# A new order for the work of a two-layer graph kernel: constants of the written-out plan changed

## The chip, the cores and the metric

The kernel runs on one core of a Trainium2 chip. The metric is the device time of one execution in microseconds (us). The core has five engines, each with its own queue that is worked off in order: PE (TensorE, matrix products), ACT (ScalarE), DVE (VectorE), POOL (GpSimd) and SP (SyncE, which here only issues DMA transfers). An engine that reaches an instruction whose inputs are not ready waits, and all that is queued behind it waits too.

## The reference

The input x has 128 batches of 128 tokens with 512 features, in float32. Two layers follow each other:

```python
# layer 0: graph maximum, residual, layer norm
A = einsum('od,bdn->bon', adj, x);  C = A + b            # per batch: adj @ x
out = max over the last axis of relu((C - A)[..., None] + A[:, :, None, :])   # one value a row
x = layernorm(x + out)
# layer 1: masked attention over the graph, projection, layer norm, residual, layer norm
q, k, v = x @ w_qkv                                      # 8 heads of 64
attn = softmax(where(adj == 0, -inf, q @ k.T / 8))
o = (attn @ v) @ w_proj + b_proj
x = layernorm(x + o + (layernorm(o) * gamma + beta))
```

Because both weights of layer 0 are adj, C - A is the bias, and the maximum over a row is relu(rowmax(adj @ x) + b).

## The kernel before

**Tiles and stages.** Batches go through in groups of four, 32 groups in all. For one batch, a tile of 128 x 512, the stages are these, with the engine and the line of the profile.

Layer 0: `load_x` (SP, L91), `conv` (PE, L186, the product with adj), `conv_max` (DVE, L190), `relu_0` (POOL, L196), then either `stats_x` (DVE, L233/L234) with `rstd_x` and `shift_x` (POOL, L240 to L250), or `add_0` and `stats_0` (ACT, L202 and L523) with `rstd_0` and `shift_0` (POOL, L213 to L225), and `norm_0` (ACT L259, or DVE L257).

Transposing x: `x_halves` splits each float into two 16-bit planes (ACT, L271) and stores them to DRAM (SP, L273, tile rowsx); `crossbar_x` reads them back with a transposing DMA (SP, L277). The tile xplanes has one buffer, so that the next `x_halves` waits for the store of the last. The four batches of the first group are transposed on PE instead (L266) and copied or split from there. `copy_x` (DVE L308 or ACT L310), `product_v` (PE, L316, in plain float32) and `keep_v` (ACT, L319) make v for batches 0 and 1.

Products in three terms: float32 operands are kept in three forms h, l and d. `split` makes the high part and l on DVE (L288, L290), `split_high` makes h (POOL L295 or ACT L297) and `split_d` makes d = h - l (POOL or DVE, both L302). Weights are split likewise by `split_w` (DVE, L150 to L152) and `split_w_rest` (ACT, L159/L160), in 16 parts (w0 to w15) that `load_w` brings in. A product then is eight matmuls of h and l (L336, L337) into one PSUM bank and four of d (L344) into another. `dense` makes q and k (indices 4 to 11) and v (0 to 3) of a group; `dense_main` (ACT, L371) and `dense_rest` (DVE, L375) add the two banks up.

Layer 1: `scores` (PE, L391), `masked` (DVE, L407), `row_max` (DVE, L416), `exps` (ACT, L425, eight instructions with their sums), `weights` (DVE, L433/L434), `halves` (ACT L440, then a store by SP, L444) and `crossbar_T` (SP, L449, a transposing DMA into eT), `attend` (PE, L471), `heads` (the split of the result o into oh, ol and od, by the lines of `split`), `project` (PE, L336 to L344), `projected_main` (DVE, L503), `projected_rest` (DVE, L517). Then the residual: a second load of x into xb (`residual`, SP, L490), `residual_x` (POOL, L494/L495) which applies the first layer's norm to it again, `residual_o` (POOL or DVE, L512). `stats` (ACT L523, POOL L529 to L538) serves both norms, `norm_1` is on DVE (L542, L517), `norm_2` on ACT (L550) with the store of the result by SP (L551). The last group transposes its softmax weights on PE (`transpose_e`) and copies them with ACT (`weights_T`, L462).

**The order.** PE's order is written out: lists of stages for the prologue, for each group and for the tail (`pro_order`, `dense_order`, `pair_order`, `tail_order`). A group's period has its q and k products first, then alternates attention of the group, v products of the group, projections of the group before, and `conv` of a group to come. Each PE stage has a length in `LENGTH`, and so a planned time. Every other stage gets a planned time as an offset from a PE stage, taken from the table `O`: four numbers, one for each batch of a group, the same for all groups in the middle; `pro` holds the times of the prologue, `tail`, `last` and `final` those of the last two groups. Flags under `two` choose between two engines or, for `project` and `dense`, between two kinds of PSUM buffer (four single banks, ps_1; two double banks, ps_2, which the scores use too). All stages are sorted by planned time and issued in that order on each engine; the planned times themselves do nothing else.

```python
at(u + O["main"][j], ...)        # a stage: planned time, function, arguments
plan.sort(key=lambda p: p[:2])   # issued in this order on every engine
```

Buffers add waits: xplanes and planes have one buffer each, e and o have three, eT, xh and xb two. A batch number in a tile's name is given by the trace where the tile belongs to one batch by name (pp_(10, 0), the product 0 of group 10; xh_('o', 36), a split of o of batch 36); tiles such as xt, xplanes, eT and e carry no number there. In this document a stage's number is its batch, and in the steady period called group 10 (from 623.43 us) the batches 36 to 39 are projected, 40 to 43 scored, and 44 to 47 normed and transposed for the next period.

Of the kernel before, what the change touches and what calls it, by code (L numbers as in the profile page):

```python
# [26 lines left out]
def tile_adj_resnorm_d2(  # L27
# [519 lines left out]
    def norm_2(b):  # L547
# [6 lines left out]

    plan, pe = [], {}
    LENGTH = dict(T=0.87, x=0.44, S=0.95, AV=0.93, conv=0.87, dense=2.82, po=2.82)
    O = {'add_0': [-38.7, -4.55, -0.42, -31.04],
 'conv_max': [2.74, 1.55, 6.27, 8.56],
 'dense_order': [('dense', 4), ('dense', 5), ('conv', 3), ('conv', 2), ('dense', 6), ('dense', 8),
                 ('dense', 7), ('dense', 11), ('dense', 10), ('dense', 9)],  # L560
 'final': {'norm_1': [5.56, 13.1, 10.45, 9.62],
           'norm_2': [10.36, 42.75, 85.51, 29.81],
           'residual': [-12.36, -9.08, -4.53, -8.07],
           'residual_o': [4.55, 8.68, 6.6, 3.13],
           'residual_x': [-31.86, -65.51, -7.05, -41.27],
           'stats_1': [5.32, 6.68, 6.06, 7.2],
           'stats_2': [7.33, 15.86, 26.2, 12.18]},
 'last': {'norm_1': [10.51, 11.91, 8.79, 8.49],
          'norm_2': [13.32, 18.89, 14.16, 15.4],
          'residual': [1.83, -2.16, 5.46, -20.9],  # L570
          'residual_o': [3.49, 5.23, 7.41, 5.77],
          'residual_x': [-44.3, 7.6, -14.48, -29.96],
          'stats_1': [3.85, 7.55, 7.55, 5.02],
          'stats_2': [10.52, 13.02, 12.74, 12.77]},
 'load': [-20.41, 3.65, -32.28, -8.94],
 'main': [4.11, 3.12, -0.15, 0.25, 3.8, -0.35, 5.39, -1.68, -0.18, -1.25, -0.35, -0.17],
 'norm_0': [13.43, 36.38, -3.62, 0.76],
 'norm_1': {'norm_1': [12.75, 21.79, 12.88, 17.03],
            'norm_2': [19.25, 33.88, 24.66, 29.53],
            'residual': [-18.48, -24.43, 1.31, 4.46],  # L580
            'residual_o': [4.44, 5.34, 5.17, 16.12],
            'residual_x': [29.52, -12.93, 5.33, 0.86],
            'stats_1': [8.25, 13.1, 5.08, 3.38],
            'stats_2': [17.35, 24.35, 16.8, 23.15]},
 'o_d': [20.5, 7.73, 4.47, 10.06],
 'o_high': [2.7, -14.24, 3.15, 9.96],
 'o_hl': [0.11, 5.8, 2.35, 8.29],
 'pair_order': [('AV', 0), ('S', 0), ('S', 1), ('AV', 1), ('dense', 0), ('po', 0), ('dense', 1),
                ('po', 1), ('S', 2), ('AV', 2), ('AV', 3), ('S', 3), ('dense', 2), ('dense', 3),
                ('po', 2), ('conv', 0), ('conv', 1), ('po', 3)],  # L590
 'po_main': [0.29, -1.52, 0.85, -1.05],
 'po_rest': [-0.11, 1.17, 1.49, 0.32],
 'pro': {'add': [-13.12, -11.18, -10.46, -7.74],
         'conv_max': [-14.78, -13.21, -11.76, -11.31],
         'copy': [-9.94, -7.2],
         'd': [-7.04, -24.39, -14.45, -43.21],
         'gamma': [38.19],
         'high': [-35.94, -5.42, -41.7, -30.01],
         'keep': [-3.31, 7.03],
         'load': [-7.74, -5.72, -1.7, 0.29],  # L600
         'norm': [-11.16, -10.47, -5.59, -6.29],
         'relu': [-14.15, -12.86, -10.61, -8.84],
         'rstd': [-13.61, -26.6, -11.53, -9.36],
         'split': [-8.15, -6.78, -11.14, -5.4],
         'stat': [-26.05, -27.35, -13.6, -11.8],
         'w': [-12.77, -7.38, 0.27, -5.64, 4.85, 5.65, 6.32, 8.94, 9.89, 9.57, 19.57, 14.52, 31.98,
               44.17, 54.64, 54.37],
         'wrest': [-28.07, -3.12, -13.69, 33.55, -0.41, 3.24, 4.95, -2.14, -20.31, 13.0, 23.61,
                   2.35, 15.05, 34.85, 35.07, 28.04]},
 'pro_order': [('conv', 0), ('conv', 1), ('conv', 2), ('conv', 3), ('x', 0), ('x', 1), ('v', 0),  # L610
               ('x', 2), ('v', 1), ('x', 3)],
 'relu_0': [-2.33, -14.2, 2.27, -8.91],
 'rest': [7.07, 3.92, 3.21, 2.37, 13.1, 2.3, 12.29, 0.25, 6.75, -0.35, 1.08, 5.26],
 'rstd_0': [21.63, -6.06, -1.85, -9.55],
 'softmax': {'cross': [-11.04, -10.0, -15.2, -5.92],
             'exps': [13.59, 24.89, 35.29, 23.69],
             'halves': [8.19, 11.44, 0.41, 1.44],
             'masked': [2.1, 1.22, 6.73, 16.85],
             'row_max': [28.59, 28.53, 20.89, 20.26],
             'weights': [9.81, 15.04, 21.31, 31.4]},  # L620
 'stats_0': [-4.77, 4.59, 27.53, -23.16],
 'tail': {'exps': [39.56, 51.32, 2.68, 7.02],
          'masked': [0.32, 0.21, 0.35, 1.14],
          'row_max': [2.8, 43.83, 0.71, 17.43],
          'weights': [8.77, 15.15, 29.55, 9.79]},
 'tail_order': [('AV', 1), ('AV', 0), ('S', 1), ('S', 0), ('dense', 0), ('dense', 1), ('po', 0),
                ('po', 1), ('S', 2), ('AV', 3), ('S', 3), ('AV', 2), ('dense', 2), ('po', 2),
                ('dense', 3), ('po', 3), ('T2', 0), ('T2', 1), ('AV2', 0), ('AV2', 1), ('po2', 0),
                ('T2', 2), ('T2', 3), ('AV2', 2), ('po2', 1), ('AV2', 3), ('po2', 3), ('po2', 2)],
 'two': {'bn': [1, 0],  # L630
         'copy': [1, 0],
         'd': [1, 1, 1, 0, 0, 1, 0, 1],
         'dense': [1, 0, 0, 0, 1, 0, 1, 0, 0, 0, 0, 0],
         'first_d': [1, 1, 1, 1],
         'first_h': [0, 0, 1, 0],
         'h': [1, 0, 0, 0, 0, 1, 0, 0],
         'norm': [0, 1, 0, 0],
         'po': [0, 0, 1, 0],
         'tail_mask': [0, 0, 0, 1],
         'tail_vector': [0, 1, 1, 1]},  # L640
 'x_cross': [-8.02, -4.16, -10.12, 2.24],
 'x_d': [7.79, -15.76, -5.19, -19.02],
 'x_halves': [-8.29, -11.6, -7.53, -6.86],
 'x_high': [-2.23, 2.47, -9.83, 1.18],
 'x_hl': [-15.93, -11.28, -4.93, -3.72]}

    def at(place, f, *a):
        plan.append((place, len(plan), f, a))
# [1 line left out]
    def two_of(kind, g, k):  # L650
        return bool(O["two"][kind][k])

    def steps():

        def dense_phase(g):
            last, far = (g - 2) * G, (g + 1) * G
            for kind, k in O["dense_order"]:
                if kind == "conv" and far < B:
# [5 lines left out]
                if g == 0 and (kind, k) == ("dense", G + 1):  # L664
                    for k in (kk for kk in range(G) if ("conv", kk) not in O["dense_order"]):
                        yield "conv", far + k

        yield from dense_phase(0)
        for g in range(NG - 1):
            for kind, k in O["pair_order"]:  # L670
                if kind in ("T", "AV", "po"):
# [5 lines left out]
                elif kind == "S":  # L677
                    yield "S", g * G + k
                elif g or ("v", k) not in O["pro_order"]:
                    yield "dense", (g, k)  # L680
            yield from dense_phase(g + 1)
        g = NG - 1
        for kind, k in O["tail_order"]:
            if kind in ("T2", "AV2", "po2"):
# [21 lines left out]
    for (kind, b), u in pe.items():  # L706
# [8 lines left out]
        tail = b >= B - G  # L715
# [4 lines left out]
        elif kind == "S":  # L720
            o = O["tail" if tail else "softmax"]
            limit = pe["T", b] if tail else pe["AV", b] - 7.0
            w = min(u + o["weights"][i], limit - 1.5)
# [20 lines left out]
        elif kind == "conv":  # L744
            at(u, conv, b)
            at(u + O["conv_max"][i], conv_max, b)
            if b >= G:
# [3 lines left out]
                cross = s + min(O["x_cross"][i], -3.0)  # L751
# [3 lines left out]
                if b ^ 1 in early:  # L755
# [13 lines left out]
                    else:  # L769
                        done = r  # L770
                        for k in pair:
                            q = min(early[k][1], limit - 2.5)
                            w = max(q + min(O["add_0"][k % G], -0.5), r + 0.1)
# [7 lines left out]
                    for k in pair:  # L781
                        n, _, _, h, cross, s, first = early[k]
                        n = max(n, done + 0.1)
                        h = max(h, n + 0.1)
                        cross = max(cross, h + 0.1)
# [56 lines left out]
    rest = [c for c in order if c >= KC]  # L842
# [48 lines left out]
```

## Time and profile before

| | us |
|---|---|
| median of 8 runs (lowest, highest) | 1973.72 (1967.98, 1977.19) |
| the profiled execution | 1974.78 |
| its span | 1973.0 |
| busy PE / DVE / ACT / POOL | 1869.0 / 1649.1 / 1548.6 / 1242.4 |
| group 0, from its first q/k product | 27.91 to 77.56 |
| group 1 | 77.56 to 151.04 |
| 28 steady groups | 151.04 to 1805.51 |
| the group before the last, and the tail | 1805.51 to 1868.33, 1868.33 to 1973.0 |

The profile page gives busy times by engine and the chain of work that ended last. The trace answers for lines, tiles and stretches of time. A row of the timeline has its start and length in us, engine, line, operation and tile; what ended the idle time before it stands in brackets. A row of the waits has the waiting instruction, what released it, the total in us, the number of times and the longest.

### The profile page before, as it was taken

What the parts mean: (1) busy time and instruction counts of PE and PEld (TensorE: products, weight loads), DVE (VectorE), ACT (ScalarE), POOL (GpSimd) and SP (SyncE); (2) the same over time, 40 slices, a digit from 0 to 9 for tenths busy, and PEclk for the clock granted to TensorE, in tenths of its full rate; (3) what the DMA queues carried; (4) which work ended last, traced back from release to release, by engine and by line L of the source; (5) the groups of instructions that cost most, each with busy time, mean ns of one, the idle gap of its engine ahead of it and who ended that gap; (6) DMA issues with size and microseconds to landing.
All of it is one profiled execution on the core that took longest, in us unless ns stands there. A gap on an engine that the chain in (4) does not pass through costs nothing.

```text
span 1973.0 us, 32988 instructions
## 1 busy us (share of the span) xinstructions
PE 1869.0 (95%) x10541; PEld 1436.0 (73%) x10541; DVE 1649.1 (84%) x2585; ACT 1548.6 (78%) x3926; POOL 1242.4 (63%) x1935
## 2 busy tenths in 40 slices
PE   6899999999999999999999999999999999999895
PEld 3677777777777777777777777777777777777774
DVE  7678888888888888888888888888888888888876
ACT  4688778788778788878788878788878788878764
POOL 3246666666666666666666666666666666667657
PEclk9899999999999999999999999999999999999998
DMA  4365565765555765555666565666555676555531
GB/s 130 102 151 158 158 161 145 174 170 159 156 161 145 176 171 161 151 159 145 176 171 161 154 156 147 174 171 165 153 160 149 166 171 167 151 159 147 147 103 64
DMA packets 486142, 302.93 MB, mean 154 GB/s; under 512 B 399440, under 2 KB 403664, under 8 KB 485969
## 3 DMA queue, kind: packets, MB, share of 16 engines
q1 hardware_dynamic: 485104, 299.70, 57.5%
q8 instruction: 84, 1.38, 0.3%
q10 hardware_dynamic: 864, 1.12, 0.2%
q14 instruction: 90, 0.73, 0.1%
HBM read 72.16 MB, written 131.07 MB: 103 GB/s over the span
## 4 chain that ended last, share of the span: by engine, by line
PE 66%; POOL 10%; DVE 8%; ACT 7%; issue 5%; DMA 4%; SPq 0%; ACTq 0%; POOLq 0%; DVEq 0%
POOL x_d L302 4%; PE psc L391 4%; PE pav L471 4%; PE pa L186 3%; DMA eT<-rows 3%; POOL od L302 2%; ACT e L425 1%; DVE x_l L290 1%; DVE v L375 1%; POOL sum L530 1%; DVE xh L288 1%; ACT xplanes L271 1%; DVE o L517 1%; ACT oh L297 1%; ACT square L523 1%
## 5 line engine op out<-in xcount | busy, mean ns | idle before, releaser
L425 ACT ACTIVATE e<-e,nmax 128x128 f32<-128x128 f32 x1016 | 393.1, 389 | 63.0 <-DVE nmax L416 63.0
L440 ACT COPY planes<-e 128x2048 uint16<-128x2048 uint16 x124 | 234.8, 1893 | 21.5 <-DVE e L434 21.4
L523 ACT ACTIVATE square<-o,sum 128x512 bf16<-128x512 f32 x256 | 183.1, 715 | 66.8 <-DVE o L517 65.8
L529 POOL TENSOR_SCALAR sum<-sum 128x1 f32<-128x1 f32 (+1 forms) x287 | 58.0, 202 | 272.7 <-ACT square L523 259.6
L495 POOL TENSOR_TENSOR xb<-xb,beta_sb 128x512 f32<-128x512 f32 x128 | 210.9, 1648 | 10.7
L302 POOL TENSOR_TENSOR x_d<-x_h,x_l 128x512 fp32r<-128x512 f32 x97 | 125.7, 1309 | 136.9 <-DVE x_l L290 98.7
L530 POOL TENSOR_TENSOR sum<-sum,mhalf 128x1 f32<-128x1 f32 (+1 forms) x287 | 180.2, 628 | 23.9
L425 ACT ACTIVATION_READ_ACCUMULATOR e<-e,nmax 128x1 f32 x1016 | 191.0, 188 | 0.0
L512 POOL TENSOR_TENSOR xb<-xb,o 128x512 f32<-128x512 f32 x125 | 164.5, 1316 | 4.9
L434 DVE TENSOR_TENSOR e<-e,sums 128x1024 f32<-128x1024 f32 x128 | 161.7, 1264 | 4.4
L542 DVE SCALAR_TENSOR_TENSOR o<-o,sum,gamma_sb 128x512 f32<-128x512 f32 x128 | 99.3, 776 | 78.8 <-POOL xb L512 73.8
L471 PE MATMUL pav<-eT,v 128*64 128x128 f32 x2048 | 139.9, 279 | 16.8 <-DMA eT<-rows 10.3
L407 DVE SCALAR_TENSOR_TENSOR e<-psc,mask 128x1024 f32<-128x1024 f32 x127 | 151.9, 1217 | 3.3 <-ACT planes L440 2.7
L416 DVE TENSOR_REDUCE nmax<-e 128x8 f32<-128x1024 f32 x127 | 153.5, 1209 | 0.1
L391 PE MATMUL psc<-qkT 64*128 64x128 f32 x2048 | 141.7, 284 | 2.4 <-DVE qkT L375 2.4
L391 PEld LDWEIGHTS psc<-qkT 64*128 64x128 f32 x2048 | 123.4, 190 | 25.7 <-issue 21.8
L494 POOL TENSOR_SCALAR xb<-xb,sum 128x512 f32<-128x512 f32 x128 | 119.7, 935 | 35.5 <-DMA xb<-in_x_dram 33.6
L550 ACT ACTIVATE o<-o,sum 128x512 f32<-128x512 f32 x128 | 103.2, 807 | 49.2 <-POOL sum L538 49.2
L471 PEld LDWEIGHTS pav<-eT,v 128*64 128x64 f32 x2048 | 110.5, 137 | 42.8 <-issue 16.0
L259 ACT ACTIVATE xt<-xt,sum 128x512 f32<-128x512 f32 x127 | 102.3, 806 | 45.9 <-POOL sum L250 44.8
L271 ACT COPY xplanes<-xt 128x1024 uint16<-128x1024 uint16 x124 | 129.7, 1046 | 5.8 <-DMA rowsx<-xplanes 2.1
L186 PE MATMUL pa<-xt,adjT 128*128 128x512 f32 x256 | 123.7, 607 | 6.6 <-ACT v L319 3.5
(4666 smaller groups left out, 5602.7 us busy)
## 6 DMA issues: line engine op xcount, KB each, us to landing
rows<-planes SPq DMA_DIRECT2D x124, 512.0 KB, 3.4
xt<-in_x_dram SPq DMA_DIRECT2D x128, 256.0 KB, 3.1
xb<-in_x_dram SPq DMA_DIRECT2D x128, 256.0 KB, 3.0
out_dram<-o SPq DMA_DIRECT2D x128, 256.0 KB, 2.9
rowsx<-xplanes SPq DMA_DIRECT2D x124, 256.0 KB, 2.4
wraw<-in_L_gnn_w_qkv_dram SPq DMA_DIRECT2D x8, 256.0 KB, 3.1
xT<-rowsx SPq DMA_TRANSPOSE x124, 3.6
eT<-rows SPq DMA_TRANSPOSE x124, 4.7
```

Of the source, the lines that this page charges most:

```text
L186: nc.tensor.matmul(pa[b], adjT, xs[b], start=True, stop=True)
L302: engine.tensor_tensor(fd, fh.bitcast(FP), fl.bitcast(FP), op=ALU.subtract)
L391: nc.tensor.matmul(psc[:, s, hp, :], qkT[hs, hp, i, :], qkT[hs, KC + hp, i, :], start=not with_mask, stop=not with_mask or hp == HP - 1,)
L416: nc.vector.tensor_reduce(nmax, src, AX.X, ALU.max, negate=True)
L425: nc.scalar.activation(e[:, j, :], src[:, j, :], AF.Exp, bias=nmax[:, j : j + 1], scale=1.0 if src is e else scale, accum_out=sums[:, j : ...
L434: nc.vector.tensor_tensor(e, e, sums[:, :, None].to_broadcast([P, H, P]), op=ALU.mult)
L440: nc.scalar.copy(planes, e.rearrange("p h m -> p (h m)").bitcast(U16).rearrange("p (m s) -> p s m", s=2),)
L471: nc.tensor.matmul(pavs[b][s * HD : (s + 1) * HD, hp, :], v[:, h * HD : (h + 1) * HD], eT[:, s * HP + hp, :], start=True, stop=True,)
L495: nc.gpsimd.tensor_tensor(xbs[b], xbs[b], beta_sb, op=ALU.add)
L512: engine.tensor_tensor(xbs[b], xbs[b], os[b], op=ALU.add)
L523: nc.scalar.activation(square, x, AF.Square, bias=s[:, 0:1], scale=-float(D), accum_out=s[:, 1:2],)
L530: nc.gpsimd.tensor_tensor(s, s, mhalf[:, :n], op=ALU.pow)
```

## The change

Only the table `O` is changed, in most of its lists, and so the planned times from which the order on each engine is sorted. No function is changed, and each instruction of the kernel stays, but for those that go to another engine by a flag. What follows from the sorting, by place:

- Prologue and group 0: the order of two convolutions on PE (0, 1, 3, 2); `rstd_x(0)` ahead of `relu_0(0)` on POOL; `norm_0(1)` and `copy_x(0)` on ACT instead of DVE; `split_d` of batches 0 and 3 on DVE instead of POOL; `split_w(10)` ahead of `split_w(9)`; `split_w_rest` parts 0, 2 and 12 elsewhere on ACT; the loads of w8, x6, w13 and w0 elsewhere on SP; `masked(2)` ahead of `split_x(7)` on DVE, `conv_max(5)` ahead of `dense_rest(0, 5)`.
- Each steady period: of a group's four projections the first takes a double bank; `residual_x` of its second batch goes forward on POOL to right behind `relu_0`; `stats` of its first batch's second norm goes ahead of `split_d` of the next group's first x on POOL; on ACT, `norm_0` of the next group's third batch goes ahead of `x_halves` of the second, and `dense_main` of v 0 ahead of `x_halves` of the third; on DVE `split_x` of the second batch goes ahead of `split_d` of the third head output; on SP one store of the result goes ahead of a transposing DMA.
- Tail: two transposing DMAs change places; `row_max(125)`, `stats(120, 1)`, `stats(120, 2)`, `heads(122)`, `norm_1(127)` and others move in their queues; on PE `attend(122)` goes ahead of `scores(127)`; `residual_o` of batches 125 and 127 is on POOL instead of DVE.

The core of the diff:

```diff
-    O = {'add_0': [-38.7, -4.55, -0.42, -31.04],
+    O = {'add_0': [-37.68, -2.23, -0.38, -6.33],
...
-           'residual_x': [-31.86, -65.51, -7.05, -41.27],
+           'residual_x': [-39.92, -69.73, -2.83, -43.83],
...
- 'main': [4.11, 3.12, -0.15, 0.25, 3.8, -0.35, 5.39, -1.68, -0.18, -1.25, -0.35, -0.17],
- 'norm_0': [13.43, 36.38, -3.62, 0.76],
+ 'main': [2.98, 2.75, -0.15, 0.6, 3.87, -0.18, 7.09, -1.59, -0.18, -1.25, -0.35, -0.17],
+ 'norm_0': [6.87, 35.07, -4.13, 0.28],
...
-            'residual_x': [29.52, -12.93, 5.33, 0.86],
+            'residual_x': [28.98, -21.86, 4.84, 3.0],
-            'stats_1': [8.25, 13.1, 5.08, 3.38],
-            'stats_2': [17.35, 24.35, 16.8, 23.15]},
+            'stats_1': [8.07, 13.05, 5.08, 3.37],
+            'stats_2': [16.98, 23.48, 16.8, 23.15]},
...
-         'keep': [-3.31, 7.03],
+         'keep': [-2.64, 6.84],
...
-         'rstd': [-13.61, -26.6, -11.53, -9.36],
-         'split': [-8.15, -6.78, -11.14, -5.4],
+         'rstd': [-16.87, -25.91, -11.45, -10.21],
+         'split': [-8.84, -6.81, -22.27, -6.08],
...
-         'w': [-12.77, -7.38, 0.27, -5.64, 4.85, 5.65, 6.32, 8.94, 9.89, 9.57, 19.57, 14.52, 31.98,
+         'w': [-12.21, -8.33, 1.74, -5.63, 4.85, 5.71, 5.4, 8.94, 9.55, 9.57, 17.31, 14.88, 32.03,
                44.17, 54.64, 54.37],
...
- 'pro_order': [('conv', 0), ('conv', 1), ('conv', 2), ('conv', 3), ('x', 0), ('x', 1), ('v', 0),
+ 'pro_order': [('conv', 0), ('conv', 1), ('conv', 3), ('conv', 2), ('x', 0), ('x', 1), ('v', 0),
                ('x', 2), ('v', 1), ('x', 3)],
...
- 'stats_0': [-4.77, 4.59, 27.53, -23.16],
+ 'stats_0': [-4.35, 2.87, 41.11, -23.16],
...
  'tail_order': [('AV', 1), ('AV', 0), ('S', 1), ('S', 0), ('dense', 0), ('dense', 1), ('po', 0),
-                ('po', 1), ('S', 2), ('AV', 3), ('S', 3), ('AV', 2), ('dense', 2), ('po', 2),
+                ('po', 1), ('S', 2), ('AV', 3), ('AV', 2), ('S', 3), ('dense', 2), ('po', 2),
...
-         'copy': [1, 0],
+         'copy': [0, 0],
...
-         'first_d': [1, 1, 1, 1],
+         'first_d': [0, 1, 1, 0],
...
-         'norm': [0, 1, 0, 0],
-         'po': [0, 0, 1, 0],
+         'norm': [0, 0, 0, 0],
+         'po': [1, 0, 1, 0],
...
-         'tail_vector': [0, 1, 1, 1]},
+         'tail_vector': [0, 0, 1, 0]},
...
- 'x_halves': [-8.29, -11.6, -7.53, -6.86],
+ 'x_halves': [-8.29, -11.6, -7.62, -6.86],
- 'x_hl': [-15.93, -11.28, -4.93, -3.72]}
+ 'x_hl': [-15.93, -11.28, -4.91, -4.16]}
```

## The prediction

> **What bounds the kernel now.** The page comes first: TensorE (PE) is busy for 1869.0 us of 1973.0, so the change can only move the remaining 104 us of PE idle time. The cut into stretches (us, then busy time of each engine, TensorE clock, DMA share, GB/s) says where that idle time lies.
>
> ```profile
> PE 1869.0 (95%) x10541; PEld 1436.0 (73%) x10541; DVE 1649.1 (84%) x2585; ACT 1548.6 (78%) x3926; POOL 1242.4 (63%) x1935
> ...
> 27.91:77.56 49.65, 42.42 (x196) 31.20 (x197) 37.39 (x59) 31.48 (x66) 12.33 (x19) 0.90 0.35 94
> 77.56:151.04 73.48, 63.42 (x331) 47.65 (x329) 54.62 (x84) 52.57 (x134) 28.00 (x39) 0.91 0.51 135
> 623.43:682.30 58.87, 57.67 (x329) 44.41 (x329) 50.34 (x80) 48.05 (x123) 38.09 (x61) 1.00 0.66 162
> 1868.33:1973.00 104.67, 79.34 (x468) 61.49 (x468) 72.88 (x117) 60.02 (x173) 70.89 (x105) 0.91 0.28 81
> ```
>
> A period runs from one group's first q/k product to the next group's. The first two have 7.2 and 10.1 us idle, a steady one (group 10 here) 1.2, the tail 25.3. From 151.04 to 1805.51 there are 28 periods in 1654.47 us, 59.09 each: 0.1 us per steady period weighs as much as 2.8 us at an end. The waits of PE name the releasers.
>
> ```profile
> PE pav L471 <- DMA eT<-rows: 10.3, 15, 1.6
> PE pp_(1, 6)_735 L336 <- DVE e L407: 6.3, 1, 6.3
> ...
> PE pa L186 <- ACT v L319: 3.5, 1, 3.5
> ...
> PE psc L391 <- DVE qkT L375: 2.4, 1, 2.4
> ```
>
> In a steady period PE waits twice: for eT, the transposed weights of the group's last batch, and at the end for od, the third form of its head outputs. In group 10 od comes 1.01 us late:
>
> ```profile
> 681.03 1.20 PE L344 MATMUL pd_('o', 39)_6858<-p_d,od 128*128 128x512 f32 x4 [1.01 <-POOL od L302]
> ```
>
> I measured in all periods where attend(39) or its like starts, as an offset a from the period's start: mean 42.29, between 41.8 and 43.5. Where a is over 42.44, the period is a + 16.42 (43.08 gives 59.50, 43.46 gives 59.88, 42.55 gives 58.98); below, a chain on DVE and POOL holds it at 58.86. So 42.44 is the point from which a later eT costs time in full. What makes eT late is ScalarE (ACT); first its timeline in group 10, then SP's:
>
> ```profile
> 653.35 0.80 ACT L259 ACTIVATE xt<-xt,sum 128x512 f32<-128x512 f32 x1
> 654.18 1.05 ACT L271 COPY xplanes<-xt 128x1024 uint16<-128x1024 uint16 x1
> ...
> 658.23 0.80 ACT L259 ACTIVATE xt<-xt,sum 128x512 f32<-128x512 f32 x1
> 659.07 1.05 ACT L271 COPY xplanes<-xt 128x1024 uint16<-128x1024 uint16 x1
> 660.02 0.59 ACT L371 ACTIVATE v<-pp_(10, 0)_6558 128x512 f32<-128x512 f32 x1
> ```
>
> ```profile
> 660.14 0.33 SPq L273 DMA_DIRECT2D rowsx<-xplanes  x1
> 660.57 1.92 SPq L449 DMA_TRANSPOSE eT<-rows  x1
> ```
>
> x_halves(46) ends at 660.12, its store is issued 0.03 later and the transpose of eT(39) 0.43 after that, because SP takes its queue in order. eT then lands 4.5 to 5.9 us on, and attend(39) starts right behind it.
>
> **The change, part by part.** The offsets in O hold for all groups, so steady periods are replanned too.
>
> *First two periods: -3.7 us (-1.5 to -4.5).* (1) norm_0(1) (0.54, L257) and copy_x(0) (0.68, L308) leave DVE, which is busy without a break from 14.56 to 27.83, for ACT, idle 3.04 us there; rstd_x(0) goes ahead of relu_0(0) on POOL. (2) split_d of batches 0 and 3 goes from POOL (1.28) to DVE (0.69). While POOL's two ran, DVE's subtraction L151 took 1.79 and 1.66 instead of 0.69, L150 1.27 instead of 0.42. Taken off: 0.46 + 0.60 by start distances, plus 1.1 of stretch; put on: 0.6 for split_d(0). The first dense product comes about 1.4 earlier. (3) On DVE the splits of weights 10 and 9 change places and on ACT keep_v(1) stands behind less of them: I follow it to 2.3 earlier, and conv(7), which waits 3.49 for it, with it. norm_0(4) comes 2.9 earlier, x_halves(6) 2.5. SP issues the loads of w8 before x4, x6 after w9, w13 before w12 and w0 earlier: the only row that waited on such a load is DVE at 34.41 (1.19), and w9 is now asked for about 1 us earlier. (4) The scores' wait of 2.42 is for DVE work behind the landing of xT(4), behind x_halves(6): so -2.5 there. (5) masked(2) fills a gap of 1.34 on DVE (73.45 to 74.79), which takes 1.2 off the DVE chain row_max(2), exps(2), halves(0), masked(3) that ends the 6.25 us wait of product (1, 6): together -3.7. conv_max(5), split_d(7), conv_max(10) and dense_main(1, 6) only change places inside that chain. Period 1's busy sums stay, so I let the gain last. Lower bound -1.5: only (1) and (2) survive; upper -4.5: (3) in full beside (5).
>
> Here a rule bears. In the trace the wait of 3.49 is followed by a clock of 0.50 from 39.4 to 43 and matmuls 0.43 apart instead of 0.23; I expect that wait to be 2.6. The Trainium skill (TensorE: Matmul & The Clock Gate, "What's actually happening") gives half clock after an idle window of about 3.4 us. By that rule the clock would stay up and PE would win some 2.8 us more there, but the scores would wait that much longer on ACT's chain, and my sum stays.
>
> *Steady periods: +9.3 us (-4 to +13.5).* (a) On ACT the order norm_0(45), x_halves(45), exps(40), norm_0(46), x_halves(46), dense_main(10, 0) becomes norm_0(45), norm_0(46), x_halves(45), exps(40), dense_main(10, 0), x_halves(46). Ahead of x_halves(46) comes dense_main(10, 0), 0.49 by start distance (660.02 to 660.51). norm_0(46) now waits for POOL L215, which ends 654.31, 0.16 after norm_0(45); the swaps give back about 0.13. x_halves(46) ends 0.52 later, and so do its store, eT(39) and a. (b) residual_x(37), two instructions on POOL (0.77 and 1.28), goes from 648.85 to right behind relu_0 at 638.8 (its load has landed at 637.07). There norm_1(35) runs on DVE, and L517 takes 0.75:
>
> ```profile
> 632.20 1.15 DVE L517 SCALAR_TENSOR_TENSOR o<-o,sum,xb 128x512 f32<-128x512 f32 x1
> ...
> 639.34 0.75 DVE L517 SCALAR_TENSOR_TENSOR o<-o,sum,xb 128x512 f32<-128x512 f32 x1
> ```
>
> The first of these lies under the same two POOL instructions (631.89 to 634.50) and took 0.40 longer. weights(39), next on DVE, would end 0.4 later than 642.67; ACT's halves(39) starts at 642.75, so 0.32 passes on: through square, POOL's stats(35, 2) and rstd to norm_0(44), then along ACT, full from 648.90 on, to x_halves(46). Bounds: 0 (no overlap) and 0.35. I take it in full, since the row has the same shapes on both engines.
>
> The mean a becomes 42.29 + 0.52 = 42.81, or 43.13 with (b): periods of 59.23 or 59.55, +0.14 or +0.46 against 59.09, +3.9 or +12.9 over 28. I take +0.33, between them and nearer the second, as the transpose's 4.5 to 5.9 us spread takes up some: +9.3. With (b) at 0.35 it is +13.5.
>
> (c) In its favour: stats(36, 2) ahead of split_d(44) on POOL, split_x(45) ahead of split_d(o38) on DVE (0.60 by start distance), and POOL free at 648.85. They bring od about 0.4 forward, but eT ends the period then. x_halves(45) starts 0.9 later; three periods now lose 0.71, 0.46 and 0.64 to a store that still reads its buffer, and that goes: -1.8. If (a) and (b) came to 0.15 together, these would leave -4, the lower end. (d) At no cost: project(36) in the double banks (its slot is the one that projected_rest(36) now frees early; covered by DVE, else a masked, 1.22, is waited for); the store of norm_2(35) ahead of the transpose of eT(38) (0.54 on SP; attend(38) has 6 us of slack); add_0 ahead of norm_2, stats(37, 2) ahead of dense_main (ACT's sum is unchanged; else 0.7).
>
> *Tail: -0.5 us (-2.5 to +2).* It hangs on POOL (70.9 us of 104.7). The loads for xb(122) and xb(123) come 0.3 later behind reordered transposes; row_max(125) behind weights(124) delays exps(125) and the square that stats(120, 1) waits for on POOL, with residual_o(120) behind it: up to 1.2, mostly in slack. Two residual_o go from DVE (0.69) to POOL (1.28 each) into the last stretch: +1.2 of POOL work where it idles. norm_1(127) comes 0.6 earlier, and the statistics that end the kernel queue 0.8 less. Sum +0.3 - 0.8.
>
> **Sum.** -3.7 + 9.3 - 0.5 = +5.1 on the profiled execution, 1974.78 (span 1973.0 and 1.8 around it), which is 1.1 above the median of eight, 1973.72: forecast 1973.72 + 5.1 = 1978.8, say 1979.
>
> **The rivals.**
> - *Absorbed.* (b) does not occur and (a) alone counts, with the vanished store waits: +3.9 - 1.8 = +2; total 1973.7 - 3.7 + 2 - 0.5 = 1971.5, and up to 1977 with half the gain at the start. For it: DVE rows near 0.98 under the same POOL work exist; against: ACT has no idle time from 648.90 to x_halves(46).
> - *Faster.* od, not eT, stays the bound and comes earlier. The mechanism is (c); its place is the end of each period, its price up to -0.4 per period. It decides once a stays under 42.3. At -4 in the steady part the total is 1965.5. For it: od is the last wait in most periods now; against: six periods in which a alone sets the length.
> - *Worse.* eT's transpose, issued later, meets the load of the next x or the planes of the next softmax and takes 5.9 rather than the middle of 5.2: +0.7 in half the periods, +10 on top: 1989. For it: the spread of a. A tail stall of 2 gives 1991.
> - *The start does not gain*: half of the ACT work moved there lands ahead of v(0): -1.5, 1981.
>
> **How the numbers follow.** The forecast with the start's variant (1977 to 1985) has 0.42, absorbed 0.25, faster 0.18, worse 0.15. 0.2% is 3.9 us, about what a measurement of this kernel can tell: same is 1969.8 to 1977.7, which takes absorbed and a little of its neighbours. Slower: 0.42 less 0.03, plus worse, plus a little of absorbed: 0.55. Range 1966 to 1990: some 4 in 10 of faster and a third of worse lie outside.
>
> **What would show it.** Right: attend(39)'s like at offsets near 43, periods of 59.4, x_halves(46) behind dense_main; L517 at 639 near 1.15; no od wait; product (1, 6) about 88. Wrong: periods of 58.5 to 58.9 with eT landing ahead of its reader, or a start that is level by 151.

## The result and the profile after

The changed kernel takes 1986.35 us (median of 12 runs, 1980.6 to 1990.84) beside 1972.31 for the kernel before (35 runs): a ratio of 1.0065, with a 95% interval of 1.0056 to 1.0075. It is slower by about 13 us. The forecast of 1979 had the direction right and its range holds the time, but its gap of 5 us is too small. A second measurement, below, gave 1.0048.

The profiled execution is the slowest of the twelve. It has a span of 1989.1 us against 1973.0, 16.1 more. The page has PE busy for 0.8 us less, so on balance the change is in idle time. Underneath, PE is busy for 2.5 us less up to period 2 and for 2.5 us more in the steady periods, which goes with the clock (below). The page's row:

```profile
PE 1868.2 (94%) x10541; PEld 1438.0 (72%) x10541; DVE 1685.9 (85%) x2583; ACT 1555.0 (78%) x3928; POOL 1271.5 (64%) x1935
```

The same four stretches as before, cut at the first q/k product of group 0, group 1, group 10, and at the tail (us, busy time by engine, clock, DMA share, GB/s):

```profile
26.99:75.16 48.17, 39.93 (x196) 29.24 (x197) 37.83 (x61) 31.54 (x67) 10.70 (x18) 0.96 0.36 98
75.16:147.49 72.33, 62.71 (x331) 47.52 (x329) 54.38 (x83) 52.26 (x134) 28.63 (x39) 0.93 0.52 138
627.00:686.42 59.42, 57.45 (x328) 44.49 (x329) 51.68 (x80) 48.23 (x123) 39.08 (x61) 1.00 0.62 160
1883.49:1989.06 105.57, 78.43 (x468) 60.53 (x468) 71.05 (x115) 60.18 (x173) 72.41 (x108) 0.92 0.29 80
```

| stretch | before | after | difference |
|---|---|---|---|
| up to period 2 | 151.04 | 147.49 | -3.55 |
| 28 steady periods | 1654.47 | 1674.80 | +20.33 |
| the group before the last | 62.82 | 61.21 | -1.61 |
| tail | 104.66 | 105.56 | +0.90 |

The start gained, as forecast, and the steady periods lost it almost six times over: 17.8 us of their 20.3 are idle time of PE, 2.5 are busy time. The waits of PE say on what (total us, times, longest):

```profile
PE pav L471 <- DMA eT<-rows: 34.4, 27, 2.8
PE pp_(1, 6)_733 L336 <- DVE e L407: 5.5, 1, 5.5
...
PE pa L186 <- ACT v L319: 3.0, 1, 3.0
```

The wait for eT went from 10.3 us in 15 places to 34.4 in 27. In group 10 the PE timeline has it, and with it the fixed wait for od at the period's end:

```profile
670.00 1.09 PE L471 MATMUL pav<-eT,v 128*64 128x128 f32 x16 [1.11 <-DMA eT<-rows]
...
685.18 1.21 PE L344 MATMUL pd_('o', 39)_6850<-p_d,od 128*128 128x512 f32 x4 [0.82 <-POOL od L302]
```

670.00 is an offset of 43.00 from the period's start at 627.00, and 43.00 + 16.42 = 59.42 is the length of the period. In the profile of after this sum holds for 23 of the 28 periods to 0.02 us. Before, it held so in six. The wait for od is a part of the 16.42: it is 0.81 to 0.83 in all 28 periods, however late eT is.

The two causes stand in the timelines of ACT and DVE. On ACT, in the same period:

```profile
657.23 0.80 ACT L259 ACTIVATE xt<-xt,sum 128x512 f32<-128x512 f32 x1
658.20 0.81 ACT L259 ACTIVATE xt<-xt,sum 128x512 f32<-128x512 f32 x1 [0.16 <-POOL sum L215]
658.92 1.03 ACT L271 COPY xplanes<-xt 128x1024 uint16<-128x1024 uint16 x1
...
662.96 0.57 ACT L371 ACTIVATE v<-pp_(10, 0)_6551 128x512 f32<-128x512 f32 x1
663.43 1.03 ACT L271 COPY xplanes<-xt 128x1024 uint16<-128x1024 uint16 x1
```

norm_0(46) waits 0.16 for POOL L215, and dense_main(10, 0) stands ahead of x_halves(46). SP issues the store at once and the transpose of eT(39) behind it:

```profile
664.49 0.33 SPq L273 DMA_DIRECT2D rowsx<-xplanes  x1
664.93 2.08 SPq L449 DMA_TRANSPOSE eT<-rows  x1
```

On DVE norm_1(35) now runs beside residual_x(37) on POOL; the first fence is DVE's timeline, the second POOL's:

```profile
642.07 0.75 DVE L542 SCALAR_TENSOR_TENSOR o<-o,sum,gamma_sb 128x512 f32<-128x512 f32 x1 [2.26 <-POOL xb L512]
642.86 1.15 DVE L517 SCALAR_TENSOR_TENSOR o<-o,sum,xb 128x512 f32<-128x512 f32 x1
```

```profile
642.30 1.16 POOL L494 TENSOR_SCALAR xb<-xb,sum 128x512 f32<-128x512 f32 x1
643.55 1.62 POOL L495 TENSOR_TENSOR xb<-xb,beta_sb 128x512 f32<-128x512 f32 x1
```

L517 takes 1.15 instead of 0.75. Offsets from the period's start, medians over the 28 periods, follow the delay along the chain:

| | before | after | difference | forecast |
|---|---|---|---|---|
| halves(39) starts | 19.33 | 19.62 | +0.29 | +0.32 |
| x_halves(46) ends | 36.69 | 37.49 | +0.80 | +0.84 |
| transpose of eT(39) issued | 37.15 | 37.96 | +0.81 | |
| attend(39) starts | 42.30 | 43.07 | +0.77 | +0.84 |
| length of the period | 58.88 | 59.50 | +0.62 | +0.33 (+0.46 by the rows) |

The transfer itself took 4.91 us from issue to landing in the median before and 4.95 after, so only 0.04 of the 0.77 is its own. The mean period grew by 0.73.

### The profile page after: what moved, and what is told of

It is laid out like the page before. It is cut to its first block, busy times and chain, and to the rows that moved or that the text cites. A ratio compares the mean times of both kernels' runs of the same rounds, so it can differ in the third digit from the quotient of the medians.

```text
span 1989.1 us, 32954 instructions
## 1 busy us (share of the span) xinstructions
PE 1868.2 (94%) x10541; PEld 1438.0 (72%) x10541; DVE 1685.9 (85%) x2583; ACT 1555.0 (78%) x3928; POOL 1271.5 (64%) x1935
## 4 chain that ended last, share of the span: by engine, by line
PE 72%; DMA 8%; DVE 7%; POOL 7%; ACT 4%; issue 2%; SPq 0%; POOLq 0%; ACTq 0%; DVEq 0%
DMA eT<-rows 7%; PE pav L471 5%; PE psc L391 5%; PE pa L186 3%; POOL od L302 2%; POOL x_d L302 2%; DVE x_l L290 1%; ACT e L425 1%; DVE ol L290 1%; DVE v L375 1%; DVE xh L288 1%; POOL sum L530 1%; POOL xb L495 1%; POOL xb L494 0%; ACT xplanes L271 0%
## 5 line engine op out<-in xcount | busy, mean ns | idle before, releaser
L302 POOL TENSOR_TENSOR x_d<-x_h,x_l 128x512 fp32r<-128x512 f32 x95 | 131.1, 1381 | 143.8 <-DVE x_l L290 102.3
L434 DVE TENSOR_TENSOR e<-e,sums 128x1024 f32<-128x1024 f32 x128 | 201.3, 1573 | 4.4
L495 POOL TENSOR_TENSOR xb<-xb,beta_sb 128x512 f32<-128x512 f32 x128 | 194.9, 1523 | 10.7
L512 POOL TENSOR_TENSOR xb<-xb,o 128x512 f32<-128x512 f32 x127 | 192.6, 1517 | 5.7 <-DVE o L517 0.9
L471 PE MATMUL pav<-eT,v 128*64 128x128 f32 x2048 | 141.0, 281 | 37.2 <-DMA eT<-rows 34.4
L542 DVE SCALAR_TENSOR_TENSOR o<-o,sum,gamma_sb 128x512 f32<-128x512 f32 x128 | 95.7, 748 | 80.4 <-POOL xb L512 74.0
L494 POOL TENSOR_SCALAR xb<-xb,sum 128x512 f32<-128x512 f32 x128 | 132.3, 1034 | 35.2 <-DMA xb<-in_x_dram 35.1
L407 DVE SCALAR_TENSOR_TENSOR e<-psc,mask 128x1024 f32<-128x1024 f32 x127 | 151.7, 1215 | 2.7 <-ACT planes L440 2.7
L517 DVE SCALAR_TENSOR_TENSOR o<-o,sum,xb 128x512 f32<-128x512 f32 x128 | 125.3, 979 | 11.1 <-POOL sum L530 1.4
```

The lines of the kernel that those rows point to most:

```text
L302: engine.tensor_tensor(fd, fh.bitcast(FP), fl.bitcast(FP), op=ALU.subtract)
L434: nc.vector.tensor_tensor(e, e, sums[:, :, None].to_broadcast([P, H, P]), op=ALU.mult)
L471: nc.tensor.matmul(pavs[b][s * HD : (s + 1) * HD, hp, :], v[:, h * HD : (h + 1) * HD], eT[:, s * HP + hp, :], start=True, stop=True,)
L495: nc.gpsimd.tensor_tensor(xbs[b], xbs[b], beta_sb, op=ALU.add)
L512: engine.tensor_tensor(xbs[b], xbs[b], os[b], op=ALU.add)
```

## The experiments

The theory was that two delays on ACT's queue, dense_main ahead of x_halves(46) and the stretched norm_1, make eT late. The rivals were other causes (the transfers, the double bank of projection 36), a start whose gain needs other parts, and a tail that loses. The second of these needs no run: in the profile of after PE never waits at a projection 36 of a steady period. On the runs' own chips the kernel before had medians between 1969.05 and 1971.84, and the transpose to eT of the last batch a median of 4.6 to 4.8 us from issue to landing instead of 4.9 in the first two profiles; ratios are always to the kernel before on the same chip.

**Each delay undone alone.** One number of the plan goes back in each run, which moves one stage in one queue.

```diff
- 'main': [2.98, 2.75, -0.15, 0.6, 3.87, -0.18, 7.09, -1.59, -0.18, -1.25, -0.35, -0.17],
+ 'main': [4.11, 2.75, -0.15, 0.6, 3.87, -0.18, 7.09, -1.59, -0.18, -1.25, -0.35, -0.17],
```

> The changed kernel with one number of its plan put back: in every period dense_main of v 0 stands behind x_halves of the third batch on ACT again, and nothing else moves. Theory (ACT's queue sets when the transpose to eT is issued, and eT sets the period): x_halves(46) ends 0.49 us earlier, at 37.0 after the period's start instead of 37.49, attend(39) starts near 42.6 instead of 43.07, periods of 59.0, the slow clock behind long waits goes: 28 x 0.49 = 13.7 and 3 x 1.5 = 4.5 us less, 1968 to 1973. Rival (the loss comes from elsewhere, the transfers or the double bank of the first projection, and ACT's order goes with it by chance): no less than 1984.

Measured: 1976.82 beside 1969.4, a ratio of 1.0032 (1.0018 to 1.0046). x_halves(46) ends at 37.03 and the median period is 59.01, as expected; the time is above the expected range. The changed kernel itself has 1.0048 with transfers as short as here (the last run below), so a third of the loss came back and not more, because 59.0 turned out to be a floor: 16 periods lie between 58.94 and 59.01 whatever their eT does, where the kernel before has its floor at 58.86. A second chain had become 0.14 longer too.

```diff
-            'residual_x': [28.98, -21.86, 4.84, 3.0],
+            'residual_x': [28.98, -12.93, 4.84, 3.0],
```

> The changed kernel with residual_x of the second batch put back behind shift_x on POOL, and nothing else moved. Theory (POOL's two instructions stretch norm_1 on DVE by 0.3, and this passes through weights, halves and the statistics to x_halves): halves(39) starts at 19.3 instead of 19.62, x_halves(46) ends at 37.2, periods of 59.2: 28 x 0.30 = 8.4 us less and one or two slow-clock periods fewer, 1974 to 1978. Rival (L517's stretch is taken up by slack on the way): 1985 to 1987.

Measured: 1971.78 beside 1969.4, 1.0009 (1.0 to 1.0019). halves(39) is back at 19.32, x_halves(46) ends at 37.18, and L517 in the timeline of DVE at the same place is short again:

```profile
637.25 0.75 DVE L517 SCALAR_TENSOR_TENSOR o<-o,sum,xb 128x512 f32<-128x512 f32 x1
```

The time is under the expected 1974 to 1978, on a chip where the kernel before is 3 us faster too. Its median period is 58.93, less than with ACT's order put back, and its shortest are 58.66, 0.2 under the floor before. So the stretch of norm_1 is a part of the eT delay and also of the second chain: masked(42) ends 49.90 after the period's start here and in the kernel before, and at 50.23 with ACT's order put back. The 0.2 under the old floor is od's: PE waits 0.81 for it, where the kernel before waits 1.0 in its periods of 58.86.

**The transpose taken out from behind the store.** SP issues eT(39) before the store of x_halves(46), so that neither delay on ACT reaches it.

```diff
- 'softmax': {'cross': [-10.24, -10.0, -13.62, -6.23],
+ 'softmax': {'cross': [-10.24, -10.0, -13.62, -11.0],
```

> The changed kernel with crossbar_T of the group's last batch planned earlier: on SP the transpose to eT(39) then stands ahead of the store of x_halves(46) instead of behind it, and nothing else moves. Theory (eT is late only because SP issues it behind that store): eT lands 4 us ahead of attend(39), that wait goes to 0 in all periods, and the period falls to what the chain to od gives: 58.86 if that chain is as before, down to 58.46 if the reordering brought od forward: 20 to 31 us less, 1955 to 1967. Rival (the transpose is late for the transfers beside it, or its longer stay on SP delays xT(44) and with it split_x): 1975 or more, with a new wait on x_l or x_h.

Measured: 1968.94 beside 1969.4, 1.0003 (0.999 to 1.0016), above the expected range. The wait for eT is gone from all steady periods, but they are 59.0 long, nearly all alike. The PE timeline of group 10 shows the second chain as a wait of its own:

```profile
666.49 0.50 PE L336 MATMUL pp_('o', 38)_6785<-p_h,oh 128*128 128x512 f32 x1 [0.64 <-DVE e L407]
...
673.94 1.21 PE L344 MATMUL pd_('o', 39)_6850<-p_d,od 128*128 128x512 f32 x4 [0.82 <-POOL od L302]
```

Projection 38 needs a double bank, which masked(42) on DVE (L407) frees. Waiting 0.64 there is what the wait for eT had hidden. I had taken od for the second limit; od's 0.82 is there in either case, and the period ends 8.71 behind the start of projection 38 (50.29 from the period's start).

The same edit on the kernel before:

```diff
- 'softmax': {'cross': [-11.04, -10.0, -15.2, -5.92],
+ 'softmax': {'cross': [-11.04, -10.0, -15.2, -11.0],
```

> The kernel before with the transpose to eT(39) ahead of the store of x_halves(46) on SP, nothing else moved. Theory (in the kernel before, a second chain holds the period at 58.86, and the change's other steady moves lower it to 58.67, as the runs with both edits showed): the wait for eT goes, the long periods go with it, the others stay at 58.86: 28 x (59.05 - 58.9) = 4 us less, 0.997 to 0.9985. Rival (the other steady moves of the change are worth nothing, and 58.67 came with the transpose's new place): 58.67 here too, 10 us less, 0.995.

Measured: 1968.21 beside 1969.05, 0.9998 (0.9989 to 1.0007). The periods stay at 58.86, as the theory says and against 58.67. The gain of 4 us is missing. The long periods did not go with the wait: six of 59.14 to 59.87 remain, together 3.9 us over 58.86. In four of them the cause is the one that the doses below show, norm_1 beside a late residual_o. With this chip's shorter transposes, the kernel before has steady periods of 59.01 to 59.05 on average in the profiles where only its start or its tail is changed, against 58.99 here, so there was 0.5 to 1.6 us to be had.

**Both edits on the changed kernel, and a third.**

> The changed kernel with both edits: the transpose to eT(39) ahead of the store of x_halves(46) on SP, and residual_x of the second batch behind shift_x on POOL. Theory: with the wait for eT gone, the periods of 59.00 came from a second chain, which the same stretch of norm_1 delays by 0.3 through halves and ACT (a wait of 0.64 for the masked of the third scores, that frees the double bank of projection 38); without the stretch that wait falls to 0.34 and the period to 58.70: 28 x 0.30 = 8.4 us less than with the transpose alone, 9 to 11 under the kernel before, about 0.995. Rival: the 0.64 is a DVE chain of its own that does not hang on halves: no gain, 59.00.

Measured: 1959.37 beside 1971.84, 0.9935 (0.9918 to 0.9952), with a median period of 58.67; this is faster than either kernel. The timeline of PE in group 10:

```profile
666.99 0.50 PE L336 MATMUL pp_('o', 38)_6785<-p_h,oh 128*128 128x512 f32 x1 [0.31 <-DVE e L407]
```

The wait halved, so this chain does hang on the stretch of norm_1: masked(42) ends 0.33 earlier, and L434 on DVE ahead of it takes 1.29 instead of 1.62. PE still waits for masked(42), so masked(42) goes ahead of split_d(o38):

```diff
- 'o_d': [21.84, 9.65, 4.95, 10.72],
+ 'o_d': [21.84, 9.65, 5.8, 10.72],
```

> The changed kernel with the transpose forward and residual_x back, and besides split_d(o38) behind masked(42) on DVE instead of ahead of it. In the run without that step PE waits 0.31 a period at projection 38, whose double bank masked(42) frees; masked(42) would end 0.6 earlier, the d part of o38 is needed only 1.9 after the projection's start. Theory: the wait goes and what follows it moves up, periods of 58.36: 28 x 0.31 = 8.7 us less than without the step, near 0.989 of the kernel before. Rival (od of batch 39 then waits longer on POOL's chain, which does not hang on projection 38): 58.67 as without it, with a wait of 1.1 instead of 0.81 at the end.

Measured: 1946.27 beside 1969.05, 0.9885 (0.987 to 0.9901), 23 us under the kernel before. The median period is 58.32. In group 10 PE waits once, for od, and the stretch has 0.95 us idle:

```profile
671.71 1.20 PE L344 MATMUL pd_('o', 39)_6850<-p_d,od 128*128 128x512 f32 x4 [0.89 <-POOL od L302]
```

```profile
614.63:672.96 58.33, 57.38 (x328) 44.36 (x329) 51.40 (x80) 48.08 (x123) 39.11 (x61) 1.00 0.64 163
```

**The delay given in doses.**

```diff
+        for _ in range((0, 2, 3, 4)[b // G % 4] if b % G == 2 and 3 * G <= b < B - G else 0):
+            nc.scalar.copy(square, square)
         planes = work.tile([P, 2, D], U16, tag="xplanes", bufs=1, name=f"xplanes_{b}")
```

> The kernel before with 0, 2, 3 or 4 useless copies of 128 x 512 (some 0.4 to 0.5 us each by start distance) on ACT ahead of x_halves of the third batch, in groups 3, 4, 5, 6 and so on in turn. Theory (period = a + 16.42 as soon as a is over 42.44, and a goes with the end of x_halves): 2 copies give a of 43.1 to 43.3 and periods of 59.6, 3 give 60.0, 4 give 60.5. And for the slow clock: waits under about 2 us cost their length alone, waits over it 1.5 us more, so some of the periods with 4 copies are 62. Rival (slack on SP or in the transpose takes a part up): a slope under half, periods of 59.2 to 59.5.

Measured: 2014.70 in one run. Four copies hold ACT for 2.46 by start distance, 0.62 each, more than I had put down; two, three and four put the end of x_halves(46) off by 1.03, 1.68 and 2.34. ACT's timeline with four:

```profile
429.61 2.56 ACT L271 COPY square<-square 128x512 bf16<-128x512 bf16 x4
```

Periods with 0, 2, 3 and 4 copies are 58.85, 60.0, 60.65 and 61.3, where no slow clock follows the wait (up to 64.8 where one does). That is 1.15, 1.80 and 2.45 more: all of the delay of x_halves(46) and 0.12 besides, and so no slack; the rival falls. But the expected sum fails: with two copies attend(39) starts at 42.9, and 42.9 + 16.42 is 59.3, not 60.0.

What the sum leaves out stands on DVE and POOL. The first fence is DVE's timeline of a period with two copies (lines of this run are two higher), the second POOL's in the same place, the third DVE's in group 10 of the kernel before, where nothing runs on POOL beside it:

```profile
320.08 1.59 DVE L519 SCALAR_TENSOR_TENSOR o<-o,sum,xb 128x512 f32<-128x512 f32 x1
```

```profile
319.37 1.76 POOL L514 TENSOR_TENSOR xb<-xb,o 128x512 f32<-128x512 f32 x1
```

```profile
669.76 0.75 DVE L517 SCALAR_TENSOR_TENSOR o<-o,sum,xb 128x512 f32<-128x512 f32 x1
```

With ACT late, residual_o on POOL comes late and lies beside this norm_1, which takes 1.56 to 1.59 instead of 0.75 in every period with copies. masked(42), behind it on DVE, ends 1.15, 1.79 and 2.45 later, and that is what the periods gained. The run bears out that ACT's time ahead of x_halves(46) is period time; in the kernel before, however, such a delay acts through DVE, and eT is not what ends the period where no slow clock follows.

The slow clock came after waits of 2.32, 2.42, 2.52 and 3.63 us for eT in periods with four copies, and not after 2.50, 2.77 and 2.89.

**The start, in two sizes.** First the three flags alone:

```diff
-         'copy': [1, 0],
+         'copy': [0, 0],
...
-         'first_d': [1, 1, 1, 1],
+         'first_d': [0, 1, 1, 0],
...
-         'norm': [0, 1, 0, 0],
+         'norm': [0, 0, 0, 0],
```

> The kernel before with the three engine flags of the first group alone: norm_0(1) and copy_x(0) on ACT, split_d of batches 0 and 3 on DVE; no planned time changed. Theory (the flags free DVE of two copies and of the stretch by POOL): the first dense product near 26.7 instead of 27.91, and most of the gain of the start: period 2 starts 1.2 to 2.5 earlier than 151.04. Rival (the order of weights and keep_v makes the gain): the first product earlier, but group 1 starts at 77.5 as before.

Measured in one run: 1970.65 beside 1971.84. The first product starts at 27.53, only 0.38 earlier, group 1 at 77.22 and period 2 at 148.19. Group 1 starts between 77.56 and 79.53 in four profiles with the order before at the start, so one profile does not tell the theory from the rival. Then the flags with the whole table of the prologue (`pro`) and its convolution order:

> The kernel before with the prologue's table, its convolution order and the three engine flags of the first group from the changed kernel: only work of the prologue and group 0 moves, periods and tail are those of before. Theory (the gain of 3.55 us at the start is the prologue's own): 3 to 3.6 us less than before, 1968.5 to 1969.5. Rival (it needs masked(2) and conv_max(5) from the changed offsets of all groups, as I forecast 1.2 us of the 3.7 from masked(2)): 2.3 less or under, 1970 to 1971.

Measured: 1967.48 beside 1969.4, 0.9986 (0.9977 to 0.9996): 1.9 us less by the medians, 2.8 by the ratio, 0.8 to 4.5 by its interval, which takes in both theory and rival. Group 1 starts at 77.23, period 2 at 147.46. Here one profile against one misleads. In four profiles with the order before at the start (before, the transpose edit, the doses, the tail) group 1 starts at 78.7 on average (77.56 to 79.53), and period 2 at 151.2 (149.55 to 152.28). In the seven of the changed kernel and its variants it is 74.9 (74.22 to 75.16) and 147.3 (144.21 to 148.66). So the whole start gains 3.8 us at group 1 and 3.9 at period 2. Of the 3.8, 1.3 are an earlier first product (26.7 on average against 28.1), and 2.4 a shorter group 0. Nearly all of the latter is PE's busy time, 40.1 us against 42.2 for the same matmuls, that is, fewer of them at a slow clock; its idle time in group 0 is 8.1 against 8.5.

The prologue's table alone brings the earlier first product (26.66), but not the shorter group 0: PE is busy there for 43.2 us in that profile, and idle for 7.4. So what it lacks is clock, and one profile does not show whether the other offsets are needed for that. In period 1 the gain neither grows nor shrinks; its length differs by up to 3 us between profiles with the same waits, by the clock (below).

**The tail alone:** the lists `final`, `last`, `tail`, `tail_order` and the flag `tail_vector`.

```diff
- 'final': {'norm_1': [5.56, 13.1, 10.45, 9.62],
+ 'final': {'norm_1': [5.87, 12.69, 9.92, 9.46],
...
-                ('po', 1), ('S', 2), ('AV', 3), ('S', 3), ('AV', 2), ('dense', 2), ('po', 2),
+                ('po', 1), ('S', 2), ('AV', 3), ('AV', 2), ('S', 3), ('dense', 2), ('po', 2),
...
-         'tail_vector': [0, 1, 1, 1]},
+         'tail_vector': [0, 0, 1, 0]},
```

> The kernel before with the changed kernel's order and flags for the last two groups alone. My forecast for this part: 0.5 us less (2.5 less to 2 more). From the profiles of the changed kernel (105.6 and 104.0 against 104.7 for the tail, 61.2 and 61.5 against 62.8 for the group before): between 1.5 less and 1 more, which five in ten thousand hardly tell from nothing: 0.999 to 1.0005. A ratio over 1.001 would say that the tail took a part of the loss.

Measured: 1971.76 beside 1969.05, 1.0012 (0.9998 to 1.0026). This is above the expected ratio, and its interval still holds no change. The profile has 108.16 us for the tail, but 82.2 of them are PE at work instead of 79.3 at a clock of 0.88 instead of 0.91; PE's idle time rose by 0.6 us only. By the interval the tail costs between nothing and 5 us; this stays open.

**The changed kernel again**, on the chip of the runs with both edits:

> The changed kernel once more, beside the three below on one chip. If eT sets its periods, its excess over the kernel before goes with how long the transposes take on this chip: ratio 1.0065 with a median of 4.95 us from issue to landing, about 1.004 (8 us) with the 4.65 to 4.70 of the runs of the second chip, since each 0.1 us in 28 periods is 2.8 us and the periods with a wait over 2 us and a slow clock become fewer. If the order of the transfers has nothing to do with it, 1.0065 again.

Measured: 1981.04 beside 1971.84, 1.0048 (1.0032 to 1.0064). x_halves(46) ends at 37.53 as before, the transposes take 4.68 in the median, attend(39) starts at 42.85, the median period is 59.28. The delay on ACT is the same to 0.04 us on both chips, and the loss follows the transfer: its median is 0.27 shorter, attend(39) and the period 0.22 each. The ratio alone would not show it, as the two intervals touch (1.0056 to 1.0075 in the first measurement).

## Why the prediction was right or wrong

**Right: the chain.** Each link of the steady part came out as worked out: the stretch of L517 (1.15, from a row of the same shapes under the same two POOL instructions), the 0.3 that it passes to halves(39), the 0.8 at x_halves(46), and the sum attend + 16.42 in the changed kernel. The rival "faster" fell, because eT, not od, ended the periods. One sign that I had named for being right did not come: "no od wait". It is 0.82 in every period and follows the start of projection 38, so it was no sign against eT.

The Trainium skill (SBUF — State Buffer, "Who interferes with whom") says that a DVE instruction with two inputs in SBUF contends with a GpSimd instruction that reads SBUF, and calls contention on the ports that the two share an exclusive lock. L517 reads o and xb from SBUF and was stretched, as the page has it: it took 0.40 longer, and POOL's two took 0.39 and 0.34 longer than in the kernel before (1.16 and 1.62 against 0.77 and 1.28). The rows do not bear out a lock for whole instructions. L517 lies beside the first of POOL's for 0.60 us and lost 0.40. Which DVE instruction cost POOL's first its 0.39 is not shown: it lies beside L542 for 0.52 us as well, and L542, which had started before it, kept its 0.75.

**Wrong: the size of the steady term.** The step that failed is "I take +0.33, between them and nearer the second, as the transpose's 4.5 to 5.9 us spread takes up some: +9.3". The rows gave +0.46 and +12.9. In the profile 25 periods have a mean of 59.51, which is +0.42 and would be +11.8 over 28, near the value that I had marked down. (On the chip with the shorter transfers the 28 periods take 1664.4 us, about 11.5 more than in the three profiles there with the steady order before.) Three more are 62.51, 62.70 and 61.90, together 8.6 us over it. There the spread, which I had let work in my favour, worked against: once eT is the last thing to come, each later landing counts in full, which is 4.0 of the 8.6: 2.9 by transfers of 5.4 to 6.3 us instead of 4.95, the rest by transposes issued 0.3 to 0.5 later. And a wait of over 2 us was followed by a slow clock, which is the other 4.6. I had carried the transfer's spread as a rival ("worse", 0.15) and not as a term.

**Wrong in part: the rule and the second limit.** The mean of a before is 42.35, not 42.29 (42.30 is the median), and the rule "period = a + 16.42 above 42.44, else 58.86" holds for 22 of the 28 periods. The other six are 0.3 to 0.7 us longer. In four of these norm_1's L517 lies beside a late residual_o and takes 1.59, as in the doses. I had no term for this second way from ACT to the period.

I named od as what holds the period when eT is early. For the kernel before this is right: its periods end at 58.86 whether projection 38 starts at 49.94 or 50.25, and the wait for od gives way, from 1.03 to 0.81. In the changed kernel od comes earlier, and masked(42), which frees the double bank of projection 38, takes its place, at 59.00 where the wait for eT gives 59.50; the stretch of norm_1 feeds both. That is why taking away one delay gave back less than its length, and why residual_x weighs more than dense_main. My (c) was right in kind, half its 0.4 in size: od's wait falls from 1.0 to 0.81, and with it the floor from 58.86 to 58.67, once the stretch is gone.

**Right in sum, wrong in its parts: the start.** -3.7 was forecast; the mean over profiles is -3.9. The first product comes 1.3 earlier over the profiles (forecast 1.4), but the three flags of my steps (1) and (2) gave 0.4 alone in one profile; the rest came with the prologue's order. conv(7) comes 1.9 earlier in the first profile of the changed kernel (forecast 2.3) and product (1, 6) 3.2 (forecast 3.7). conv(7)'s wait became 3.01 (forecast 2.6). I had given the clock no part in the sum ("my sum stays"); the shorter group 0 is 2.1 us of faster matmuls. So the sum is right partly by luck.

**Tail.** -0.5 was forecast; the one profile has +0.9, with -1.6 in the group before; alone it measures 1.0012 with an interval that includes nothing. Not settled.

## What to carry to other kernels

A transfer in an in-order queue starts when the instruction ahead of it is issued: look what the late transfer stands behind before shortening it. Here one place further ahead took its wait away, and the next chain was 0.5 us a period below (0.3 with the shorter transfers), so it took three edits, each at a wait or a stretch that the runs had laid bare, to reach 0.9885. A late engine can also push work of a third one beside the chain that ends last: here ACT's delay put POOL's residual_o beside DVE's norm_1, which then took twice as long. When a delay reaches a chain that already ends last in some periods, count it in full and add the spread of the transfer; do not mark it down.

## What was not expected of the hardware

The TensorE clock fell after shorter waits than I had reckoned with. Four stretches of the changed kernel, two waits for eT and the 3.1 us behind each (the clock stands ahead of the last two numbers):

```profile
606.67:609.05 2.38, 0.01 (x1) 0.03 (x1) 2.35 (x6) 2.35 (x4) 2.05 (x3) 1.00 1.17 117
609.05:612.20 3.15, 3.15 (x32) 2.64 (x32) 2.93 (x4) 1.82 (x2) 2.94 (x2) 0.63 0.99 306
1207.83:1209.76 1.93, 0.00 (x1) 0.03 (x1) 1.90 (x5) 1.90 (x3) 1.76 (x3) 1.00 1.12 220
1209.76:1212.90 3.14, 3.14 (x36) 2.68 (x37) 2.92 (x5) 2.09 (x2) 1.78 (x2) 1.00 1.08 277
```

A wait of 2.38 us was followed by a clock of 0.63 and cost 1.5 us more; one of 1.93 by 1.00 and nothing. Over five profiles, waits for eT of 2.08, 2.14, 2.16, 2.32 (twice), 2.38, 2.42, 2.46, 2.52, 2.81, 3.04 and 3.63 were followed by a slow clock, those of 2.02, 2.05, 2.39, 2.50, 2.77 and 2.89 were not, and none up to 1.93 was. In period 1 two waits of 1.2 and 1.4 us with four matmuls (L344) between them are followed by a slow stretch in some executions and not in others. The kernel before, whose waits there are the same to 0.02 us in its variants, has that period between 70.2 and 73.6 us for this. The Trainium skill (TensorE: Matmul & The Clock Gate, "What's actually happening") gives half clock after an idle window of about 3.4 us; here 2.08 us was enough and 2.89 was not, so a wait of over 2 us is a risk rather than a threshold. The first group's wait for keep_v does not follow the page's figure either. Behind 3.49 to 3.62 us the clock was 0.50 to 0.58 in four profiles of the kernel before and its variants and full in a fifth (the tail's, 3.53); behind 3.01 it was full in five profiles of the changed kernel and its variants and 0.58 and 0.64 in two; behind 2.51, with the prologue's table alone, it was 0.53.
